# Five pairs of nodes instead of four in each PSUM tile of edge counts, and layer 0 woven in after every third tile

## The chip, the cores and the metric

The kernel runs on one core of a Trainium2 chip. The metric is the device time of one execution in microseconds (us). A core has a matrix engine (PE, whose weight loads are listed as PEld), a vector engine (DVE), a scalar engine (ACT), a general engine (POOL), and an engine that here only issues transfers (SP). Each engine works through its own queue in the order in which the program was compiled; they wait for one another by semaphores.

## The reference

The inputs are 6250 nodes of 128 features and 206,250 edges, sorted by their destination. Four graph layers follow one another, each after a layer norm and a ReLU, and each added to the residual `x`:

```python
h = relu(layernorm(x))
neighbor = segment_sum(edge_weight[:, None] * h[src], dst, N)       # layer 0
x = x + leaky_relu(neighbor @ W1.T + b1 + (h * neighbor) @ W2.T + b2, 0.2)
h = relu(layernorm(x))
agg = segment_sum(h[src], dst, N) / max(degree, 1)                  # layer 1
f = gelu(agg @ Wl.T + bl + h @ Wr.T)
...                                         # f is normalised over all nodes, f + h added to x
summed = segment_sum(x_clique[dst], src, N)                         # layer 2, a mean
x = x + (summed / max(count, 1)) @ W.T + b
h = relu(layernorm(x)) @ W_in.T + b_in                              # layer 3, a GRU cell
agg = segment_sum((h @ W_msg)[src], dst, N)
x = x + gru(agg, h) @ W_out.T + b_out
```

All four need sums over the same edges. What matters here is only the first: for each node, a sum over its edges of a weight times a row of `h`.

## The kernel before, in words

The kernel turns the list of edges into dense matrices and multiplies by them. The 6250 nodes are 49 blocks of 128 (`NB` = 49, `P` = 128). For every block of destinations two matrices over all 49 x 128 sources are made: `cnt`, how many edges lead from a source to a destination (bf16), and `edge_w`, the sum of their weights (f32). Layer 0 multiplies by `edge_w` at once; `cnt` goes to HBM (`cnt_d`, and turned by DMA for the first 25 blocks, `cntT_d`) and is read back by layers 1 to 3, in the second half of the kernel (`dense`, L820). That half is not edited.

The first half is a loop over 25 **strips** of two blocks, the last of one block (L793). For each strip:

- `prepare(k)` (L623) finds the edges of each node with gathers from HBM that POOL issues (`fetch`, L620): first a line of the sorted list (`line`), then twice up to 64 edges of a node (`dst`, `src`, `wgt`), one half after the other since the second half begins where the first one ends. DVE compares what lands (`same`, L657) and computes the next offset `off_i` (L652). The edges' fields are then turned so that an edge lies on a partition (PE, L675) and copied to `by_edge` (ACT, L677). This runs a strip or more ahead of its use.
- `count(k, ...)` (L680) makes the two matrices. A **pair** is two nodes, with up to 64 edges each, on 64 partitions each. DVE writes **one-hots** for 16 pairs at a time (`TW` = 16): `s_hot` (L695) says which of the 128 nodes of its block an edge's source is, and `k_hot` (L697, L699) which of the 49 blocks, once plainly and three times multiplied by a part of the weight. The pool `hot` has two buffers of each. PE multiplies them (L712): for each pair six products of 64 edges, three on each half of the array, into one PSUM tile `pK`. A `pK` tile is two banks, one for each node of the pair, and a pair takes 2 x 49 columns in each: 49 for the count, 49 for the weights. There are three `pK` buffers. `PW` = 4 pairs fill a tile; ACT then copies the counts to `cnt` (L726) and the weights to `edge_w` (L727).
- `layer0(k, ...)` (L743) multiplies `h0` by `edge_w`, 49 products of 128x256 f32 (L748), each of which is two instructions in the profile. It is a generator that stops after every six of them. What follows the 49 products is a chain of small steps: a copy by ACT (L753), products (L756, L762, L763), several DVE steps (L758, L765 to L771), a norm (L549), transposes of `h1` (L779) and a last product (L785, L787).

Layer 0 of one strip is **woven** into the counting of the next: whenever `count` yields, the driver asks `layer0` for its next **slice** of six products. The few lines that do it:

```python
for _ in count(k, nb, ready.pop(0), edge_w):
    next(before, None)
for _ in before:
    pass
before = layer0(k, nb, edge_w)
```

`count` yields once for each set of one-hots, which is 16 pairs or four `pK` tiles, so eight times in a strip. The tail of layer 0 comes out after the strip's last yield. In strip 0, where there is no earlier strip, `before` is the generator `norms` instead, which makes `h0`. A planner orders the instructions of each engine at compile time: near a strip's change it mixes layer 0's tail with the first tiles of the next strip, and it places `prepare`'s steps between the one-hots in DVE's queue.

When a block is complete, SP issues its write to `cnt_d` (L735), and for the first 25 blocks also seven transposing DMAs with their writes (L740, L741). `cnt` has two buffers.

Of the kernel before, what the change touches and what calls it, by code (L numbers as in the profile page):

```python
# [11 lines left out]
BF16 = mybir.dt.bfloat16  # L12
AF = mybir.ActivationFunctionType
ALU = mybir.AluOpType
DVE = mybir.EngineType.DVE

P = 128
D = 128
N = 6250
NB = -(-N // P)  # L20
# [444 lines left out]
WN = 2  # L465
H = P // WN
SB = 2
# [2 lines left out]
NS = len(STRIPS)  # L470
TW = 16
TI = 2
PW = 4
CB = 4
NQB = -(-NQ // P)
CHUNKS = [(g, min(CB, n - g)) for b, n in ((0, NQB), (NQB, NB)) for g in range(b, n, CB)]
# [9 lines left out]
def fast(ctx: ExitStack, tc: tile.TileContext, a: dict, out: bass.AP, flag: bass.AP):  # L486


    nc = tc.nc
# [35 lines left out]
    cnt_d = dram.tile([NCH, P, CB, NB * P], BF16, name="cnt_d")  # L525
# [11 lines left out]
    def flat(t):  # L537
        return t.rearrange("p b f -> p (b f)")
# [42 lines left out]
    with ExitStack() as bx:  # L581
        def pool(name, bufs):
            return bx.enter_context(tc.tile_pool(name="b_" + name, bufs=bufs))
# [12 lines left out]
        iota = keep.tile([P, P, TI], BF16, name="iota")  # L596
# [16 lines left out]
        pay, hot, work = pool("pay", 2), pool("hot", 2), pool("work", 1)  # L613
        edge = pool("edge", 2)
        cnts, turned, once = pool("cnts", 2), pool("turned", 3), pool("once", 1)
# [7 lines left out]
        def prepare(k):  # L623
# [53 lines left out]
            nc.scalar.copy(by_edge, pv)  # L677
            return by_edge

        def count(k, nb, by_edge, edge_w):  # L680


            mats = []
            for t0 in range(0, nb * P // WN, TW):
                tq = TW // TI

                def at(i, n):
                    v = by_edge[:, i, t0 : t0 + TW].rearrange("p (q o t) -> p q o t", o=1, t=TI)
                    return v.to_broadcast([P, tq, n, TI])

                def count_up(n):
                    return iota[:, None, :n, :].to_broadcast([P, tq, n, TI])

                s_hot = hot.tile([P, tq, P, TI], BF16, name="s_hot")
                nc.vector.tensor_tensor(s_hot, count_up(P), at(0, P), op=ALU.is_equal)  # L695
                k_hot = hot.tile([P, 4, tq, NB, TI], BF16, name="k_hot")
                nc.vector.tensor_tensor(k_hot[:, 0], count_up(NB), at(1, NB), op=ALU.is_equal)  # L697
                for i in range(1, 4):
                    nc.vector.tensor_tensor(k_hot[:, i], k_hot[:, 0], at(1 + i, NB), op=ALU.mult)  # L699
                for q in range(0, TW, PW):  # L700

                    pk = psum.tile([P, WN, 512], F32, name="pK", bufs=3)
                    for i in range(PW):
                        (u, t), o = divmod(q + i, TI), 2 * NB * i
                        for j in (0, 2, 3):
                            for h in range(WN):
                                r = slice(h * H, (h + 1) * H)
                                if j:
                                    to, rhs = slice(o + NB, o + 2 * NB), k_hot[r, j, u, :, t]
                                else:  # L710
                                    to, rhs = slice(o, o + 2 * NB), k_hot[r, :2, u, :, t]
                                nc.tensor.matmul(pk[:, h, to], s_hot[r, u, :, t], rhs, start=j == 0,  # L712
                                                 stop=True, skip_group_check=True)
                    n0 = (t0 + q) * WN
                    nn = PW * WN
                    if n0 % P == 0:
                        mats.append(cnts.tile([P, NB, P], BF16, name="cnt"))

                    def by_block(half):
                        v = pk[:, :, : 2 * PW * NB].rearrange("p h (i c b) -> p c b i h", c=2, b=NB)  # L720
                        return v[:, half]

                    def to_nodes(m):
                        return m.rearrange("p b (i h) -> p b i h", h=WN)

                    nc.scalar.copy(to_nodes(mats[n0 // P][:, :, n0 % P : n0 % P + nn]), by_block(0))  # L726
                    nc.scalar.copy(to_nodes(edge_w[:, :, n0 : n0 + nn]), by_block(1))  # L727
                yield
                n0 = (t0 + TW) * WN
                if n0 % P:  # L730
                    continue
                j = n0 // P - 1
                g = k * SB + j
                c, i = CHUNK_OF[g]
                nc.sync.dma_start(cnt_d[c, :, i, :], flat(mats[j]))  # L735
                if g >= NQB:
                    continue
                for q in range(0, NB, 7):
                    tt = turned.tile([P, 7, P], BF16, name="tt")
                    nc.sync.dma_start_transpose(tt, flat(mats[j][:, q : q + 7, :]))  # L740
                    nc.sync.dma_start(cntT_d[:, g, q * P : (q + 7) * P], flat(tt))  # L741

        def layer0(k, nb, edge_w):  # L743
# [49 lines left out]
        for k, nb in STRIPS:  # L793
            if k + 1 < NS:
                ready.append(prepare(k + 1))
            edge_w = edge.tile([P, NB, SW], F32, name="edge_w")
# [5 lines that stand above are left out]
# [89 lines left out]
    for g in range(0, NQB, GB):  # L891
        nb = min(GB, NQB - g)
        xq = work.tile([P, GB, D], F32, name="xq")
        n = min(NQ - g * P, nb * P)
# [80 lines left out]
    for g, nb, acc in dense(q_parts, False):  # L975
# [21 lines left out]
        h = work.tile([P, CB, D], F32, name="wb")  # L997
# [12 lines left out]
        for j in range(nb):  # L1010
            nc.tensor.matmul(pm[:, j * D : (j + 1) * D], hh[:, (g + j) * P : (g + j + 1) * P],  # L1011
                             w_msg, start=True, stop=True)
# [5 lines left out]
    for g, nb, acc in dense(m_parts, True):  # L1018
# [13 lines left out]
        r, z = gates  # L1032
# [14 lines left out]
        for j in range(nb):  # L1047
            o = po[:, j * D : (j + 1) * D]
# [13 lines left out]
def gnn_kernel(tc: tile.TileContext, a: dict, out: bass.AP):  # L1062
    nc = tc.nc
    with tc.tile_pool(name="flag", bufs=1) as keep:
        flag = keep.tile([1, 1], I32, name="flag")
        fast(tc, a, out, flag)
        found = nc.values_load(flag[0:1, 0:1], min_val=0, max_val=2 * E,
                               skip_runtime_bounds_check_because="a count of edges, each at most twice")
        with tc.If(found != E):
            general(tc, a, out)  # L1070
# [48 lines left out]
```

## Time and profile before

| | before |
|---|---|
| median of 3 runs | 2252.22 us (2247.76 to 2259.28) |
| the profiled execution's own time | 2246.41 us |
| its span, first to last instruction | 2244.6 us |
| its mean granted TensorE clock | 0.956 |
| first counting product (L712) | 53.2 us after the start |
| last strip's write of `cnt` (L735) | 1256.2 us after the start |
| strip with transposes and gathers, 234.8 to 284.3 us | 49.5 us |
| strip with gathers only, 924.2 to 971.0 us | 46.8 us |
| strip with neither, 1112.0 to 1155.6 us | 43.6 us |

A strip's time here runs from one transposition of edge fields (L675) to the next. In the profile, a group is a line of the kernel with the engine, the operation, the tiles that it writes and reads, the number of instructions, their busy time, the mean of one in ns, and the idle time of the engine just ahead of them with what ended it. A wait is read "engine, line, what it waited for: us in total, times, longest". "issue" is idle time for which the profile shows no cause. A busy share is a mean over stages with different limits, so it says little on one edit; the timeline of the stage does.

### The profile page before, as it was taken

How to read it: one execution, taken by the hardware profiler on the slowest of the kernel's cores; microseconds unless marked ns; L12 is line 12 of the kernel's file. 1: busy time of each engine (PE TensorE's matmuls, PEld its weight loads, DVE VectorE, ACT ScalarE, POOL GpSimd, SP SyncE). 2: the span in 40 equal slices, each digit the busy share in tenths (PEclk: the TensorE clock that was granted, in tenths of full speed). 3: DMA queues.
4: the chain of work that ended last, by engine and by line, in shares of the span. 5: the costliest groups of instructions: out<-in, count | busy, mean ns of one | idle time of the engine just before them, and what ended most of it. 6: DMA issues, size and time to landing. Idle time of an engine off the chain costs nothing. (4 is left out here: it accounts for less than half of the span.)

```text
span 2244.6 us, 60368 instructions
## 1 busy us (share of the span) xinstructions
PE 1959.0 (87%) x25624; PEld 1573.7 (70%) x25624; DVE 1412.1 (63%) x3349; ACT 1182.8 (53%) x2692; POOL 344.9 (15%) x377
## 2 busy tenths in 40 slices
PE   0568988888898889998999859999969989999998
PEld 0457776777777777777777747888756767778776
DVE  6687676666666666666766267777785554443443
ACT  1645555555555565665666336666645455443443
POOL 4431122211111221111100020000041110000000
PEclk9989999999999999999999979999989899997999
DMA  3687899888898222223222398878846668775774
GB/s 62 160 159 185 220 202 211 219 200 217 206 204 220 93 80 95 80 87 88 80 98 80 121 257 292 266 240 276 258 140 205 205 204 271 243 237 165 241 236 139
DMA packets 423787, 406.32 MB, mean 181 GB/s; under 512 B 191216, under 2 KB 414307, under 8 KB 417235
## 3 DMA queue, kind: packets, MB, share of 16 engines
q1 hardware_dynamic: 414883, 394.35, 61.1%
q0 software_dynamic: 5600, 6.56, 1.2%
q8 instruction: 203, 3.33, 0.6%
q10 hardware_dynamic: 3024, 1.45, 0.4%
q14 instruction: 77, 0.63, 0.1%
HBM read 227.26 MB, written 134.89 MB: 161 GB/s over the span
## 5 line engine op out<-in xcount | busy, mean ns | idle before, releaser
L726 ACT CAST cnt<-pK 128x392 bf16<-128x392 f32 x784 | 402.8, 514 | 399.5 <-PE pK L712 299.7
L748 PE MATMUL pL<-edge_w,h 128*128 128x256 f32 (+1 forms) x2450 | 610.1, 399 | 0.3 <-ACT agg L753 0.3
L712 PE MATMUL pK<-k_hot,s_hot 64*128 64x49 bf16 (+1 forms) x18816 | 429.6, 195 | 124.7 <-issue 68.9
L712 PEld LDWEIGHTS <-s_hot 64*128 64x128 bf16 x18816 | 370.6, 96 | 217.7 <-issue 166.2
L748 PEld LDWEIGHTS pL<-edge_w,h 128*128 128x128 f32 x2450 | 462.4, 200 | 66.3 <-ACT agg L753 0.5
L727 ACT COPY edge_w<-pK 128x392 f32<-128x392 f32 x784 | 410.2, 523 | 0.0
L852 PE MATMUL acc<-some,parts 128*128 128x512 f32 (+1 forms) x1456 | 374.5, 399 | 27.6 <-DVE some L847 19.7
L695 DVE TENSOR_TENSOR s_hot<-iota,by_edge 128x2048 bf16<-128x2048 bf16 x196 | 240.0, 1225 | 188.4 <-PE pK L712 180.4
L852 PEld LDWEIGHTS acc<-some,parts 128*128 128x128 f32 x1456 | 273.7, 196 | 92.9 <-DVE some L847 25.1
L699 DVE TENSOR_TENSOR k_hot<-k_hot,by_edge 128x784 bf16<-128x784 bf16 x588 | 309.5, 577 | 5.2
L841 ACT CAST others<-ring 128x1536 fp32r<-128x1536 bf16 (+3 forms) x156 | 192.4, 1233 | 206.7 <-PE acc L852 143.0
L840 DVE CAST some<-ring 128x2048 fp32r<-128x2048 bf16 (+3 forms) x156 | 166.9, 1071 | 182.8 <-PE acc L852 172.1
L852 PE MATMUL acc<-others,parts 128*128 128x512 f32 (+1 forms) x1092 | 280.1, 391 | 0.0
L847 DVE TENSOR_SCALAR_CACHE_REDUCE some<-ring 128x512 fp32r<-128x512 bf16 (+1 forms) x364 | 216.3, 652 | 63.2 <-PE acc L852 38.3
L852 PEld LDWEIGHTS acc<-others,parts 128*128 128x128 f32 x1092 | 205.2, 195 | 42.1 <-issue 0.5
L850 ACT ACTIVATE others<-ring 128x512 fp32r<-128x512 bf16 (+1 forms) x273 | 162.3, 597 | 109.9 <-issue 53.7
L774 POOL TENSOR_TENSOR xs<-xs,h 128x256 f32<-128x256 f32 (+1 forms) x25 | 26.9, 1075 | 798.0 <-ACT h L565 755.1
L852 PE MATMUL acc<-some,q_parts 128*128 128x512 f32 (+1 forms) x390 | 114.8, 422 | 31.7 <-DVE some L840 31.7
L852 PEld LDWEIGHTS acc<-some,q_parts 128*128 128x128 f32 x390 | 73.7, 204 | 53.0 <-DVE some L840 37.1
L697 DVE TENSOR_TENSOR k_hot<-iota,by_edge 128x784 bf16<-128x784 bf16 x196 | 110.2, 562 | 0.0
L657 DVE TENSOR_SCALAR_CACHE_REDUCE same<-dst,node 128x64 bf16<-128x64 int32 x50 | 13.9, 277 | 119.6 <-DMA dst<-in_dst,off_i 116.3
L852 PE MATMUL acc<-others,q_parts 128*128 128x512 f32 (+1 forms) x260 | 81.0, 422 | 0.0
(155 smaller groups left out, 1526.1 us busy)
## 6 DMA issues: line engine op xcount, KB each, us to landing
ring<-cnt_d SPq DMA_DIRECT2D x168, 896.0 KB
cnt_d<-cnt SPq DMA_DIRECT2D x49, 1568.0 KB
cntT_d<-tt SPq DMA_DIRECT2D x175, 224.0 KB
ring<-cntT_d SPq DMA_DIRECT2D x60, 640.0 KB
ring<-cnt_d SPq DMA_DIRECT2D x14, 224.0 KB
xs<-in_x SPq DMA_DIRECT2D x24, 128.0 KB
xs<-in_x SPq DMA_DIRECT2D x12, 256.0 KB
u_d<-xs SPq DMA_DIRECT2D x24, 128.0 KB
```

The source lines that it names most:

```text
L695: nc.vector.tensor_tensor(s_hot, count_up(P), at(0, P), op=ALU.is_equal)
L697: nc.vector.tensor_tensor(k_hot[:, 0], count_up(NB), at(1, NB), op=ALU.is_equal)
L699: nc.vector.tensor_tensor(k_hot[:, i], k_hot[:, 0], at(1 + i, NB), op=ALU.mult)
L712: nc.tensor.matmul(pk[:, h, to], s_hot[r, u, :, t], rhs, start=j == 0, stop=True, skip_group_check=True)
L726: nc.scalar.copy(to_nodes(mats[n0 // P][:, :, n0 % P : n0 % P + nn]), by_block(0))
L727: nc.scalar.copy(to_nodes(edge_w[:, :, n0 : n0 + nn]), by_block(1))
L748: nc.tensor.matmul(pl[:, :w], h0[:, s, :], edge_w[:, s, :w], start=s == 0, stop=s == NB - 1)
L840: nc.vector.tensor_copy(some[:, :dve, :nb], t[:, :dve])
L841: nc.scalar.copy(others[:, : step - dve, :nb], t[:, dve:])
L847: nc.vector.tensor_scalar(rhs, t[:, i], 1.0, None, op0=ALU.mult, op1=ALU.add, accum_out=total)
L850: nc.scalar.activation(rhs, t[:, i], AF.Copy, accum_out=total)
L852: nc.tensor.matmul(acc[:, :w], parts[:, q + i, j, :], rhs, start=q + i + j == 0, stop=q + i + j == last)
```

## The change

A `pK` tile takes five pairs in place of four (`PW` = 5), which is 490 of a bank's 512 columns. A block has 64 pairs (`WB`), so it is now counted in 13 tiles, twelve of five pairs and one of four, in place of 16. Tiles no longer end where one-hots do: the one-hots, still for 16 pairs each, are made by a function `one_hots` at the first pair that needs them, and a tile may read two sets.

`count` now yields after the third, sixth, ninth and thirteenth tile of a block, so the slices of layer 0 stand after 15, 30, 45 and 64 pairs in place of 16, 32, 48 and 64. There are still eight yields in a full strip. `cnt` is allocated at the start of a block. The products, their number and their order within a pair stay as they are, as do the sizes of all pools.

```diff
-PW = 4
+PW = 5
+WB = P // WN
...
+        def one_hots(by_edge, t0):
...
+            s_hot = hot.tile([P, tq, P, TI], BF16, name="s_hot")
+            nc.vector.tensor_tensor(s_hot, count_up(P), at(0, P), op=ALU.is_equal)
+            k_hot = hot.tile([P, 4, tq, NB, TI], BF16, name="k_hot")
+            nc.vector.tensor_tensor(k_hot[:, 0], count_up(NB), at(1, NB), op=ALU.is_equal)
+            for i in range(1, 4):
+                nc.vector.tensor_tensor(k_hot[:, i], k_hot[:, 0], at(1 + i, NB), op=ALU.mult)
+            return s_hot, k_hot
+
         def count(k, nb, by_edge, edge_w):
-            mats = []
-            for t0 in range(0, nb * P // WN, TW):
...
-                for q in range(0, TW, PW):
+            hots, banks = {}, range(0, WB, PW)
+            for j in range(nb):
+                g, cnt = k * SB + j, cnts.tile([P, NB, P], BF16, name="cnt")
+                for m, w0 in enumerate(banks):
+                    n = min(PW, WB - w0)
                     pk = psum.tile([P, WN, 512], F32, name="pK", bufs=3)
-                    for i in range(PW):
-                        (u, t), o = divmod(q + i, TI), 2 * NB * i
+                    for i in range(n):
+                        q, t = divmod(j * WB + w0 + i, TW)
+                        if q not in hots:
+                            hots[q] = one_hots(by_edge, q * TW)
+                        (s_hot, k_hot), (u, t), o = hots[q], divmod(t, TI), 2 * NB * i
...
-                    nc.scalar.copy(to_nodes(mats[n0 // P][:, :, n0 % P : n0 % P + nn]), by_block(0))
-                    nc.scalar.copy(to_nodes(edge_w[:, :, n0 : n0 + nn]), by_block(1))
-                yield
+                    nc.scalar.copy(to_nodes(cnt[:, :, of]), v[:, 0])
+                    nc.scalar.copy(to_nodes(edge_w[:, :, slice(j * P + of.start, j * P + of.stop)]), v[:, 1])
+                    if m + 1 == len(banks) or m % 3 == 2 and m + 2 < len(banks):
+                        yield
```

In the changed kernel the lines of this stage move: the counting products are L722 (before L712), the copies L730 and L731 (L726, L727), the one-hots L693, L695 and L697 (L695, L697, L699), and the lines of `prepare` are one higher (the comparison of a gather L658 in place of L657). From L735 on the numbers are the same.

More of the change, by code (lines that the diff above doesn't have):

```diff
@@ L678, in prepare @@
             return by_edge
-        def count(k, nb, by_edge, edge_w):
-            mats = []
-            for t0 in range(0, nb * P // WN, TW):
[L685 to L699, printed above, removed]
-                for q in range(0, TW, PW):
-                    pk = psum.tile([P, WN, 512], F32, name="pK", bufs=3)
-                    for i in range(PW):
-                        (u, t), o = divmod(q + i, TI), 2 * NB * i
-                        for j in (0, 2, 3):
@@ new lines, in one_hots, with at, count_up @@
+        def one_hots(by_edge, t0):
+            tq = TW // TI
+            def at(i, n):
+                v = by_edge[:, i, t0 : t0 + TW].rearrange("p (q o t) -> p q o t", o=1, t=TI)
+                return v.to_broadcast([P, tq, n, TI])
+            def count_up(n):
+                return iota[:, None, :n, :].to_broadcast([P, tq, n, TI])
+            s_hot = hot.tile([P, tq, P, TI], BF16, name="s_hot")
[5 more added lines that the diff above has]
+            return s_hot, k_hot
@@ new lines, in count @@
+        def count(k, nb, by_edge, edge_w):
+            hots, banks = {}, range(0, WB, PW)
[3 more added lines that the diff above has]
+                    n = min(PW, WB - w0)
+                    pk = psum.tile([P, WN, 512], F32, name="pK", bufs=3)
+                    for i in range(n):
[3 more added lines that the diff above has]
+                        (s_hot, k_hot), (u, t), o = hots[q], divmod(t, TI), 2 * NB * i
+                        for c in (0, 2, 3):
@@ L706, in count @@
                             for h in range(WN):
                                 r = slice(h * H, (h + 1) * H)
-                                if j:
-                                    to, rhs = slice(o + NB, o + 2 * NB), k_hot[r, j, u, :, t]
+                                if c:
+                                    to, rhs = slice(o + NB, o + 2 * NB), k_hot[r, c, u, :, t]
                                 else:
                                     to, rhs = slice(o, o + 2 * NB), k_hot[r, :2, u, :, t]
-                                nc.tensor.matmul(pk[:, h, to], s_hot[r, u, :, t], rhs, start=j == 0,
+                                nc.tensor.matmul(pk[:, h, to], s_hot[r, u, :, t], rhs, start=c == 0,
@@ L713, in count @@
                                                  stop=True, skip_group_check=True)
[L714 to L721, printed above, removed]
+                    of = slice(w0 * WN, (w0 + n) * WN)
@@ L723, in to_nodes @@
+                    v = pk[:, :, : 2 * n * NB].rearrange("p h (i c b) -> p c b i h", c=2, b=NB)
                     def to_nodes(m):
                         return m.rearrange("p b (i h) -> p b i h", h=WN)
-                    nc.scalar.copy(to_nodes(mats[n0 // P][:, :, n0 % P : n0 % P + nn]), by_block(0))
-                    nc.scalar.copy(to_nodes(edge_w[:, :, n0 : n0 + nn]), by_block(1))
-                yield
-                n0 = (t0 + TW) * WN
-                if n0 % P:
-                    continue
@@ L732, in count @@
-                j = n0 // P - 1
-                g = k * SB + j
+                    nc.scalar.copy(to_nodes(cnt[:, :, of]), v[:, 0])
+                    nc.scalar.copy(to_nodes(edge_w[:, :, slice(j * P + of.start, j * P + of.stop)]), v[:, 1])
+                    if m + 1 == len(banks) or m % 3 == 2 and m + 2 < len(banks):
+                        yield
                 c, i = CHUNK_OF[g]
-                nc.sync.dma_start(cnt_d[c, :, i, :], flat(mats[j]))
+                nc.sync.dma_start(cnt_d[c, :, i, :], flat(cnt))
@@ L739, in count @@
                     tt = turned.tile([P, 7, P], BF16, name="tt")
-                    nc.sync.dma_start_transpose(tt, flat(mats[j][:, q : q + 7, :]))
+                    nc.sync.dma_start_transpose(tt, flat(cnt[:, q : q + 7, :]))
                     nc.sync.dma_start(cntT_d[:, g, q * P : (q + 7) * P], flat(tt))
```

## Prediction

> **What bounds the kernel now.** I read the page's busy times and slices first: the counting stage runs from 53 to about 1290 us, and only this stage is edited. Then the groups, the list of waits, and the timelines of PE and DVE over two strips.
>
> ```profile
> PE 1959.0 (87%) x25624; PEld 1573.7 (70%) x25624; DVE 1412.1 (63%) x3349; ACT 1182.8 (53%) x2692; POOL 344.9 (15%) x377
> L726 ACT CAST cnt<-pK 128x392 bf16<-128x392 f32 x784 | 402.8, 514 | 399.5 <-PE pK L712 299.7
> L748 PE MATMUL pL<-edge_w,h 128*128 128x256 f32 (+1 forms) x2450 | 610.1, 399 | 0.3 <-ACT agg L753 0.3
> L712 PE MATMUL pK<-k_hot,s_hot 64*128 64x49 bf16 (+1 forms) x18816 | 429.6, 195 | 124.7 <-issue 68.9
> ```
>
> The stage is mostly PE: 429.6 us of counting products plus 610.1 us of layer 0 in some 1240 us. ACT waits for PE (299.7 us), not the reverse. What PE loses stands in the waits (engine, line, waited for: us, times, longest):
>
> ```profile
> PE pK L712 <- issue: 68.9, 123, 2.0
> PE pK L712 <- ACT edge_w L727: 45.5, 162, 5.2
> PE pD L779 <- ACT h L565: 20.9, 24, 3.0
> DVE same L657 <- DMA dst<-in_dst,off_i: 116.3, 40, 5.7
> ```
>
> The second line is the edit's target. In the PE timeline (start, us, then the idle time in brackets) one round of 16 pairs and six products of layer 0 looks so:
>
> ```profile
> 942.43 1.39 PE L712 MATMUL pK<-k_hot,s_hot 64*128 64x98 bf16 x72
> 944.02 0.58 PE L712 MATMUL pK<-k_hot,s_hot 64*128 64x98 bf16 x24 [0.21 <-ACT edge_w L727]
> 944.53 2.86 PE L748 MATMUL pL<-edge_w,h 128*128 128x256 f32 x12
> 947.32 1.39 PE L712 MATMUL pK<-k_hot,s_hot 64*128 64x98 bf16 x72
> ```
>
> Three tiles run through, the fourth waits 0.16 to 0.25 us for the first to be drained, the slice of layer 0 takes 2.79 us, and the round is 4.89 us. DVE, making the one-hots of a later round, meets a gather in the early part of a strip:
>
> ```profile
> 974.36 1.22 DVE L695 TENSOR_TENSOR s_hot<-iota,by_edge 128x2048 bf16<-128x2048 bf16 x1 [1.35 <-PE pK L712]
> 975.50 0.56 DVE L697 TENSOR_TENSOR k_hot<-iota,by_edge 128x784 bf16<-128x784 bf16 x1
> 979.05 0.28 DVE L657 TENSOR_SCALAR_CACHE_REDUCE same<-dst,node 128x64 bf16<-128x64 int32 x1 [2.99 <-DMA dst<-in_dst,off_i]
> 979.25 1.51 DVE L699 TENSOR_TENSOR k_hot<-k_hot,by_edge 128x784 bf16<-128x784 bf16 x3
> ```
>
> Here k_hot is late by the wait for the gather; PE does not feel it, since it needs this k_hot only at 984.60.
>
> **What the skill says.** "ScalarE: Activation LUTs", section "What ACT_TABLE_LOAD costs", gives 186 ns + 0.833 ns per element, with back-to-back instructions overlapping by about 93 ns. The trace agrees: 392 elements would be 513 ns (measured 514), copies from PSUM of 256 and 512 elements took 372 and 586 ns, a slope of 0.836, and evictions start 0.377 us apart where they take 0.48 to 0.57. "PSUM — Partial Sum Buffer", section "The four PSUM rules", gives a bank 512 fp32 columns: five pairs take 5 x 98 = 490 and fit; the kernel before shows only 392. "DVE: scalar operands, raw-bit mode, write accounting and state across instructions", section 5, calls the DVE's queue in-order; the lines above show it, k_hot behind L657.
>
> **The change, part by part.** Call a strip's time zero T, the start of its five transposes L675 (971.0 and 433.3 in two strips). Pairs cost PE 1.87/16 = 0.117 us each.
>
> Evictions. 784 pairs of copies become 49 x 13 = 637. One of 490 starts (490-392) x 0.836 = 82 ns later after its predecessor, 0.459 us. For a block ACT goes from 32 x 0.377 = 12.06 to 24 x 0.459 + 2 x 0.377 = 11.77 us. ACT is idle 299.7 us behind PE, so this 0.29 us counts for nothing by itself.
>
> Waits on the drain. Eight waits in a strip, 1.36 us (12.7 us over nine strips in 760-1180). After, groups of 3, 3, 3 and 4 tiles: the first three never meet a busy buffer. The fourth does: the first tile of 30 products ends after 0.585 us, ACT starts 0.14 later and its second copy ends 0.459 + 0.57 us after that, 1.75 us; PE is through with three tiles at 1.76. So about 0.05 us is left, twice a strip. One more deduction: the first group after a strip's change is followed by L779, which waits 0.80 us for h, a chain DVE-ACT that starts from L763 and stays. What PE saves in that group (0.20 us) and the pair that moves out of it (0.117 us) is waited for there and paid again in the 19-pair group. Net: 1.36 - 0.10 - 0.20 - 0.117 = **0.94 us a strip without gathers**.
>
> One-hots that straddle. A one-hot tile still serves 16 pairs and has two buffers, but the slices now fall after pairs 15, 30, 45, 64. Its buffer is given back at pair 16, and the refill is needed at pair 32: before, 2.79 + 1.87 + 2.79 = 7.5 us later; now one slice and 16 pairs, 2.79 + 1.87 = 4.7 us, three times in four. DVE needs 1.14 + 0.59 + 3 x 0.48 = 3.2 us, about 3.45 from release. 1.2 us of slack: free in the plain rounds (covered by PE's own rounds), not where a gather is in the way. The changed program's DVE order says where: third one-hot, then L662, L667, L670 and L655, **then the wait on the gather (L658), and only then the whole fourth one-hot**, where before s_hot and a quarter of k_hot stood ahead of it. POOL's and SP's queues keep their order.
>
> Walk for a later strip (gather lands at T+8.1). PE: pair 29 done at T+2.1, slice to 4.85, pair 44 at 6.6, slice to 9.4, pair 47 at 9.74. The third one-hot is ready at 4.2, needed at 5.1. Fourth: L658 done 8.4, s_hot and k_hot with two off_i between 8.6 to 12.05. PE stops **about 2.2 us**. But before, PE lost in the same place about 3 us to "issue" gaps, which stand beside the gathers' issue on POOL (976.72 to 983.48): 1.4 us at T+6.5 to 8.5, the rest after T+9, the second partly inside a slice. After, the first window falls into a slice and the stop. PE restarts at 12.1, does 16 pairs and a slice: 16.75 plus 0 to 1.5 us of the second window. Before, this point was T+18.46 and T+17.9. So 0 to 1.5 us less, I take 0.6, and the strip's other four groups save 0.6: **1.2 us a strip**, six strips.
>
> First half (transposes L740 run, gather lands at about T+10). The fourth one-hot is ready at 13.9, a stop of 4 us; the second gather is asked for 0.25 us later than now, and the fifth one-hot is ready at 19.8 to 20.8. PE comes there at 19.1 plus gaps; before it came at T+20.3 and T+22.1, the gaps having taken the same time. So 0 here, 0.6 saved after: **0.6 us**, 13 strips. SP's queue has room: it waited 23.2 us for ACT's cnt over eight strips.
>
> Strip 0, without layer 0, waits 15 us for ACT (11 waits) mostly behind norms: 2 us less, bounds -6 to +4 as its DVE order is reshuffled. The straddling itself adds no instruction.
>
> Sum: 4 x 0.94 + 6 x 1.2 + 13 x 0.6 + 2 = 3.8 + 7.2 + 7.8 + 2 = **21 us** off the profiled execution's 2246.4 us (span 2244.6): 0.93%. That execution lay 0.26% under the median, 2252.2; the same share of the median gives **2231 us**. Everything after 1290 us stays.
>
> **The rivals.**
> A, slower: the fourth one-hot's wait adds to the gaps instead of covering them. Place: pair 48 of each strip with gathers; price 2.2 us in six strips, 4 us in thirteen, less the 0.6 saved behind: 9.6 + 44 - 6 = +48 us, 2300. It decides as soon as the gaps lost at T+6 to T+17 reappear in full after PE's restart. For it: L657's 116.3 us and the slack of 1.2 us. Against: the gaps sit at the gathers' own times.
> B, better: PE's stop lets its instructions catch up, so the gaps go too: 1.5 us more in nineteen strips, about -50 us, 2202. For it: strips without gathers take 43.6 us, others 46 to 52.
> C, the first half gives all back, to the gathers or to the transposes' queue (DMA share 0.89 there): only 3.8 + 7.2 + 2 = 13 us, 2239. For it: there the point at pair 64 hangs on the second gather either way.
> That the tile is not larger is excluded: the program's evictions read 49x10.
>
> **Numbers.** Forecast 0.50, C 0.20, A 0.17, B 0.13. A measurement of this kernel tells about 0.5%, 11 us, from no change: under 2241 is faster, over 2263 slower. Forecast nine tenths, B whole and C in part give faster 0.65; C's rest and the forecast's edge 0.18; A 0.17. Range 2204 to 2266: it holds the forecast and C with the first half's bounds (each 0.5 us a strip), and leaves out most of A above and half of B below.
>
> **What would show it.** Waits of pK on edge_w from 45.5 to under 18 us, two a strip, each under 0.1 us. A new or larger wait of pK on k_hot (9.6 us now), about 2 us a strip late and 4 early, once per strip near T+10. "issue" before pK falling from 68.9 us. Strips without gathers at 42.6 us in place of 43.6. Eviction mean near 595 ns. Wrong if waits on k_hot pass 60 us with the issue gaps unchanged (A), or if waits on edge_w stay above 30 us: then the drain, not the count of buffers, sets the pace.

## The result, and the profile after

The changed kernel takes 2276.76 us, median of five runs (2273.17 to 2276.95), against 2256.18 of the kernel before in the same session (2247.76 to 2261.19). The ratio is 1.0092, 95% interval 1.0066 to 1.0118. It is slower by 0.9%, with an interval clear of 1: on the other side of no change from the forecast of 2231, and above the range of 2204 to 2266. The profiled execution took 2276.36 us, span 2274.6.

The groups of the page that answer to those shown of before:

```profile
PE 1933.9 (85%) x25624; PEld 1566.5 (69%) x25624; DVE 1402.4 (62%) x3349; ACT 1161.1 (51%) x2398; POOL 362.3 (16%) x377
L748 PE MATMUL pL<-edge_w,h 128*128 128x256 f32 (+1 forms) x2450 | 611.9, 399 | 0.4 <-ACT agg L753 0.3
L722 PE MATMUL pK<-k_hot,s_hot 64*128 64x49 bf16 (+1 forms) x18816 | 420.6, 198 | 153.7 <-DVE k_hot L697 129.7
```

PE is busy for 25 us less than before and the kernel takes 30 us more, so over the whole kernel the time went into waiting. In the list of waits (engine, line, waited for: us, times, longest):

```profile
PE pK L722 <- DVE k_hot L697: 129.7, 109, 6.7
DVE less L638 <- DMA line<-in_dst,at_i: 64.7, 17, 6.0
PE pD L762 <- DVE inter L758: 25.2, 23, 1.1
PE pK L722 <- ACT edge_w L731: 14.3, 16, 3.8
PE pK L722 <- issue: 5.4, 6, 3.4
```

The edit did what it says: the wait for a drained buffer fell from 45.5 to 14.3 us, and all that is left of it stands in the first 124 us. The gaps called "issue" went too, from 68.9 to 5.4. In their place stands a wait for one-hots, 9.6 us before and 129.7 now. The second line, 15.0 us before, points at one cause of it.

By strips, each measured from one transposition of edge fields (L675, now L676) to the next:

| part of the counting stage | before, us | after, us |
| --- | --- | --- |
| up to the first of the strips below | 184.9 | 176.6 |
| eight strips with transposes and gathers | 401.0 | 445.1 |
| the four after them, in which the transposes end | 199.1 | 204.2 |
| five strips with gathers only | 233.1 | 234.0 |
| the last strip with all its gathers | 50.4 | 54.1 |
| three strips with neither | 130.9 | 128.3 |
| start of the last transposition | 1199.3 | 1242.3 |

At the last transposition 43 us are lost. The eight strips lose 44, since each takes 55.6 us in place of 50.1; the strips between them and the last three lose 10 more, and 11 are gained at the two ends. One of the eight, from its start at 399.7, in the timeline of DVE (start, us, instruction, idle time before it):

```profile
415.75 1.22 DVE L693 TENSOR_TENSOR s_hot<-iota,by_edge 128x2048 bf16<-128x2048 bf16 x1
416.89 0.56 DVE L695 TENSOR_TENSOR k_hot<-iota,by_edge 128x784 bf16<-128x784 bf16 x1
423.42 0.29 DVE L638 TENSOR_SCALAR less<-line,f_node 128x128 bf16<-128x128 int32 x1 [5.97 <-DMA line<-in_dst,at_i]
423.62 1.51 DVE L697 TENSOR_TENSOR k_hot<-k_hot,by_edge 128x784 bf16<-128x784 bf16 x3
```

and of PE:

```profile
412.42 0.27 PE L722 MATMUL pK<-k_hot,s_hot 64*128 64x98 bf16 x2 [2.96 <-DVE k_hot L697]
424.24 0.22 PE L722 MATMUL pK<-k_hot,s_hot 64*128 64x98 bf16 x2 [4.09 <-DVE k_hot L697]
```

The fifth one-hot is begun at 415.75, but `less`, a comparison for a later strip, stands in DVE's queue in the middle of it. DVE waits there 5.97 us for a gather, and PE behind it 4.09. Each of the eight strips has this wait of 5.9 to 6.0 us. The first PE line is the fourth one-hot's stop, which was forecast.

Why the gather is late is in the timelines of POOL and SP. After:

```profile
415.91 1.88 POOL L621 DMA_INDIRECT line<-in_dst,at_i  x1 [1.48 <-DVE same L658]
```

```profile
417.14 0.32 SPq L735 DMA_DIRECT2D cnt_d<-cnt  x1
```

and before, with DVE's own lines last:

```profile
397.93 0.94 POOL L620 DMA_INDIRECT line<-in_dst,at_i  x1 [0.30 <-DMA f_d<-fs]
```

```profile
402.65 0.32 SPq L735 DMA_DIRECT2D cnt_d<-cnt  x1
```

```profile
402.23 0.29 DVE L637 TENSOR_SCALAR less<-line,f_node 128x128 bf16<-128x128 int32 x1 [1.70 <-DMA line<-in_dst,at_i]
402.43 1.52 DVE L699 TENSOR_TENSOR k_hot<-k_hot,by_edge 128x784 bf16<-128x784 bf16 x3
```

Before, the gather is issued at 397.93 and compared at 402.23, 4.3 us later, the longest of the eight strips, and the 1.57 MB of a block's count leave for HBM only at 402.65. After, the block ends earlier beside the gather, the write is issued 1.2 us behind it, and the gather takes 7.5 us.

The distance of 1.2 us is only half of it. The other half is the second number of the POOL lines: the issue of this gather took 1.88 us in each of the eight strips, against 0.94 before, so the write was issued before the gather's issue had ended. The records of single DMA packets in the trace give the order: the write's packets start at 417.95, and those of the gather only at 421.61, when the write's last ones start. In the next strip after the eight the write follows at 1.06 us, closer still, but the issue took 0.94 us, the gather's packets were first, and the comparison began 2.6 us after the issue. The long issues fell on DVE's one-hots: all of the 17 gather issues of more than 1.3 us in this trace ran beside one, as did all 24 before. That is a coincidence in time, and no run here parts it from a cause.

The stops seem to have a second price. In the stretch from 200 to 600 us (length, then busy us and instructions of PE, PEld, DVE, ACT and POOL, granted PE clock, DMA share, GB/s) the mean granted clock fell from 0.96 before to 0.88 after:

```profile
200.00:600.00 400.00, 351.38 (x7079) 288.13 (x7079) 270.62 (x596) 226.04 (x560) 80.05 (x93) 0.96 0.88 210
200.00:600.00 400.00, 323.02 (x6402) 270.30 (x6403) 242.85 (x537) 195.43 (x415) 81.14 (x84) 0.88 0.76 189
```

The trace's clock records show why the mean fell: in the eight strips the clock was granted at 0.5 for 31 us in 8 steps before, and for 96 us in 16 steps after, two a strip. Of these 16, 13 begin within 1.4 us of the end of a PE stop of more than 1.3 us. Of the 44 us lost, 35 are longer waits of PE and 8 are longer busy time. That the stops bring the clock down is read from this coincidence, not tested alone.

### The profile page after: what moved, and what is told of

Its sections match the earlier page's. It is cut to its first block, busy times and chain, and to the rows that moved or that the text cites. A ratio compares the mean times of both kernels' runs of the same rounds, so it can differ in the third digit from the quotient of the medians.

```text
span 2274.6 us, 59963 instructions
## 1 busy us (share of the span) xinstructions
PE 1933.9 (85%) x25624; PEld 1566.5 (69%) x25624; DVE 1402.4 (62%) x3349; ACT 1161.1 (51%) x2398; POOL 362.3 (16%) x377
## 5 line engine op out<-in xcount | busy, mean ns | idle before, releaser
L730 ACT CAST cnt<-pK 128x490 bf16<-128x490 f32 (+1 forms) x637 | 372.6, 585 | 472.8 <-PE pK L722 359.0
L722 PE MATMUL pK<-k_hot,s_hot 64*128 64x49 bf16 (+1 forms) x18816 | 420.6, 198 | 153.7 <-DVE k_hot L697 129.7
L722 PEld LDWEIGHTS <-s_hot 64*128 64x128 bf16 x18816 | 376.6, 98 | 235.7 <-issue 127.1
L852 PE MATMUL acc<-some,parts 128*128 128x512 f32 (+1 forms) x1456 | 365.6, 392 | 32.5 <-DVE some L847 20.0
L731 ACT COPY edge_w<-pK 128x490 f32<-128x490 f32 (+1 forms) x637 | 379.9, 596 | 0.0
L852 PEld LDWEIGHTS acc<-some,parts 128*128 128x128 f32 x1456 | 268.0, 191 | 95.2 <-DVE some L847 22.4
L693 DVE TENSOR_TENSOR s_hot<-iota,by_edge 128x2048 bf16<-128x2048 bf16 x196 | 240.9, 1229 | 140.5 <-PE pK L722 137.9
L697 DVE TENSOR_TENSOR k_hot<-k_hot,by_edge 128x784 bf16<-128x784 bf16 x588 | 302.9, 569 | 4.6
L847 DVE TENSOR_SCALAR_CACHE_REDUCE some<-ring 128x512 fp32r<-128x512 bf16 (+1 forms) x364 | 216.1, 651 | 59.4 <-PE acc L852 38.4
L774 POOL TENSOR_TENSOR xs<-xs,h 128x256 f32<-128x256 f32 (+1 forms) x25 | 17.9, 716 | 815.0 <-ACT h L566 815.0
L695 DVE TENSOR_TENSOR k_hot<-iota,by_edge 128x784 bf16<-128x784 bf16 x196 | 114.2, 583 | 0.0
L658 DVE TENSOR_SCALAR_CACHE_REDUCE same<-dst,node 128x64 bf16<-128x64 int32 x50 | 13.7, 275 | 106.3 <-DMA dst<-in_dst,off_i 106.3
```

The costliest lines, as they stand in the source:

```text
L730: nc.scalar.copy(to_nodes(cnt[:, :, of]), v[:, 0])
L731: nc.scalar.copy(to_nodes(edge_w[:, :, slice(j * P + of.start, j * P + of.stop)]), v[:, 1])
L847: nc.vector.tensor_scalar(rhs, t[:, i], 1.0, None, op0=ALU.mult, op1=ALU.add, accum_out=total)
L852: nc.tensor.matmul(acc[:, :w], parts[:, q + i, j, :], rhs, start=q + i + j == 0, stop=q + i + j == last)
```

## The experiments

The theory after the first look: `less`, waiting for `line` inside a one-hot, costs the eight strips (the **line theory**). Rivals: the two one-hots made back to back at a strip's end, which push L758 and so L762, PE's wait for `inter` (the **inter theory**), and the straddling one-hots with two buffers, which leave DVE less time to refill one (the **lead theory**). The letters in the expectations are each its own: the "theory L" of the first and the fourth run is the lead theory. Each ratio is against the kernel before in the same session.

**One-hots and slices on the same pairs.** Five pairs to a tile stay, but a slice comes ahead of each new one-hot, after 16, 32, 48 and 64 pairs.

```diff
                         if q not in hots:
+                            if hots and (w0 or i):
+                                yield
                             hots[q] = one_hots(by_edge, q * TW)
...
-                    if m + 1 == len(banks) or m % 3 == 2 and m + 2 < len(banks):
+                    if m + 1 == len(banks):
```

> Five pairs to a tile as in the changed kernel, but the slices of layer 0 stand where a set of one-hots ends (pairs 16, 32, 48, 64), inside a tile if need be. DVE's order is then that of the kernel before. Theory L (what costs is the shortened time between a one-hot buffer's return and its refill, with gathers in DVE's queue; the drain's gain is real): waits of pK on edge_w under 15 us (45.5 before, 14.3 after), waits of pK on k_hot at 10 us as before, waits of L764 on inter back from 25 to 9 us; time 2215 to 2240, faster than both. Rival D (the drain's gain is not real, PE only meets its issue gaps sooner): waits on edge_w gone, issue gaps up by as much, time 2250 to 2260, that of the kernel before.

Measured: 2222.94 us, ratio 0.9874 (0.9839 to 0.9909). Its waits:

```profile
PE pK L724 <- DVE k_hot L697: 69.8, 97, 7.1
PE pK L724 <- ACT edge_w L733: 34.2, 86, 4.6
DVE less L638 <- DMA line<-in_dst,at_i: 15.9, 13, 4.3
```

The time was hit, two of the three waits were not: the drain's wait is back at 34.2 us, and yet this kernel is about 2% faster than the changed one by the two ratios. So the drain is not what this difference hangs on. L762's wait returned to 0.30 us a strip, `line` to 15.9 us in all (15.0 before) and the lead to that of before, all at once, so this run doesn't part the three theories.

It shows something else, in a strip that starts at 370.1:

```profile
384.39 0.94 POOL L621 DMA_INDIRECT line<-in_dst,at_i  x1 [0.30 <-DVE at_i L634]
385.09 0.32 SPq L737 DMA_DIRECT2D cnt_d<-cnt  x1
387.54 0.28 DVE L638 TENSOR_SCALAR less<-line,f_node 128x128 bf16<-128x128 int32 x1 [0.19 <-DMA line<-in_dst,at_i]
```

The write follows the gather by 0.7 us in all eight strips, and the comparison still begins 3.0 to 3.3 us after the gather's issue, which took 0.94 us. In the ninth strip the write goes 0.8 us ahead of the gather, and it is 6.6 us. A write close behind a gather is thus not enough to make it late; in these runs it has to get ahead.

**The group of four tiles first** (4, 3, 3, 3 in place of 3, 3, 3, 4), which parts the two one-hots at the strip's end:

```diff
-                    if m + 1 == len(banks) or m % 3 == 2 and m + 2 < len(banks):
+                    if m + 1 == len(banks) or m % 3 == 0 and m > 0:
```

> The changed kernel with its groups in the order 4, 3, 3, 3 tiles, slices at pairs 20, 35, 50, 64, so that the last two one-hot buffers of a strip are given back with a slice between them. Theory I (the 1.1 us wait of L762 on inter, 25.2 us against 8.9, comes from two one-hots in a row ahead of L758, and delays the whole strip): L762 waits fall to about 9 us and the time by 10 to 20 us, to 2257 to 2267; waits of pK on k_hot stay over 100 us. Rival (that wait is hidden by later ones, above all by those on the gathers): L762 waits fall, time stays within 5 us of 2277.

Measured: 2260.79 us, ratio 1.0036 (1.0014 to 1.0058). The time lies in the inter theory's range, but not by its mechanism: L762's wait fell to 7.0 us as meant, and L779's rose from 22.5 to 38.4, so this wait mostly only moves. The gain came with the wait for `line`, which fell from 64.7 to 18.8, and stands in the eight strips (412.3 us in place of 445.1); what follows them up to the last transposition grew from 620.5 to 629.8. Waits of pK on k_hot fell to 93.3, under the 100 expected.

**No gather of the line.**

```diff
-            line = once.tile([P, P], I32, name="line")
-            fetch(line, "dst", at_i)
+            line = line_once
```

> The changed kernel without the gather of line: the comparison less reads a constant tile, so the edges found are not those of the nodes, and the count of edges that decides on the second program is set by hand. Theory G (in the first eight full strips the fifth one-hot waits 5.9 us in DVE's queue behind L638, which waits for line): waits of pK on k_hot fall from 130 to 70 to 90 us, strips of the first half from 55.3 to 50 to 51.5 us, time 2230 to 2245. Rival T (the first half is held by the transposes and their queue, and line is only the nearest wait): strips stay over 54 us, the wait turns up at cnt or elsewhere, time 2265 or more.

Measured: 2197.34 us, ratio 0.9756 (0.9722 to 0.9790); the eight strips take 388.9 us. The gain on the changed kernel is about twice the expected one: 56 us in the eight strips and 13.5 at the beginning. L762's wait for `inter` stayed at 25.4 us, so the inter theory can't explain the loss. The line theory can, but with the gather go its load and the edges that it finds.

**Eight pairs to a one-hot, four buffers:** `TW` = 8 in place of 16, `pool("hot", 4)`.

> The changed kernel with one-hots for 8 pairs and four buffers of each in the same space, so that a buffer is given back after 8 pairs and refilled for use 24 pairs later. Theory L (lead time): a refill has 24 pairs and one or two slices, 5.6 to 8.4 us, for about 1.8 us of DVE work; waits of pK on k_hot fall from 130 to under 60 us, time 2225 to 2250. Rival Q (DVE's queue order is what costs: behind the gather's comparison stands the next one-hot whatever its size): waits on k_hot stay over 100 us, time 2270 or more; twice as many DVE instructions also cost about 0.3 us for 16 pairs.

Measured: 2244.30 us, ratio 0.9973 (0.9952 to 0.9995). The time was hit; waits of pK on k_hot, at 98.9 us, were not. The five strips with gathers only fell to 42.2 to 43.8 us, but the first half's stayed at 53.8 to 55.1 with 78.7 us of waits of `less`. The lead is worth something where the line is not in the way.

**The line compared and counted on GpSimd**, so that DVE's queue has no wait for it:

```diff
-            nc.vector.tensor_scalar(less, line, n0, None, op0=ALU.is_lt)
-            nc.vector.tensor_reduce(c, less, axis=mybir.AxisListType.X, op=ALU.add)
-            nc.vector.tensor_add(off, at, c)
+            nc.gpsimd.tensor_scalar(less, line, n0, None, op0=ALU.is_lt)
+            w = P // 2
+            while w:
+                nc.gpsimd.tensor_tensor(less[:, :w], less[:, :w], less[:, w : 2 * w], op=ALU.add)
+                w //= 2
+            nc.gpsimd.tensor_tensor(off, at, less[:, :1], op=ALU.add)
```

It was put into four kernels: the changed one, the one with aligned slices, the one with small one-hots, and the one before.

> The changed kernel with the comparison and the count of line (L638, L640, L642) done by POOL in place of DVE; every gather is still issued. Theory G (it is the place of this wait in DVE's queue that costs): strips of the first half from 55.3 to 48 to 50 us as in e3, waits of pK on k_hot 70 to 100 us, time 2200 to 2225. Rival H (the gather itself costs, by its traffic or by the edges that e3 no longer found, wherever its result is read): strips stay at 53 us or more, time 2255 or more.

> e1 with line compared on POOL. In e1 DVE waited only 15.9 us for line. Theory G: 5 to 20 us less than e1, 2203 to 2218. Rival: in e1 this wait was hidden behind the second gather of dst, time within 4 us of e1's 2223.

> e4 with line compared on POOL. In e4 the strips of the second half had come down to 42.2 to 43.8 us while those of the first half stayed at 54 to 55 us behind waits for line (78.7 us). Theory G: first-half strips at 46 to 49 us, waits of pK on k_hot under 50 us, time 2165 to 2200, the fastest of all. Rival T (first-half strips are held by the transposes, DMA share near 0.9): they stay at 52 us or more, time 2225 or more.

> The kernel before with line compared on POOL, so that the edit of e5 is seen without the change. DVE waited 15.0 us for line there, ten times. Theory G (the wait costs only where the one-hots have lost their lead): 0 to 15 us less than the kernel before, 2236 to 2251. Rival H (it costs in any kernel): 40 us less or more, below 2212.

| kernel | us | ratio | eight strips, us | they start at |
| --- | --- | --- | --- | --- |
| changed, line on GpSimd | 2231.58 | 0.9894 (0.9863 to 0.9926) | 392.1 | 190.1 |
| aligned, line on GpSimd | 2242.32 | 0.9937 (0.9917 to 0.9956) | 402.3 | 188.4 |
| small one-hots, line on GpSimd | 2207.62 | 0.9782 (0.9749 to 0.9816) | 386.5 | 203.8 |
| before, line on GpSimd | 2237.67 | 0.9930 (0.9908 to 0.9953) | 398.0 | 195.0 |

Here the gather is still made, and the eight strips of the changed kernel fall by 53 us with the comparison off DVE's queue, those of the kernel before by 3. The line theory is shown, and the 44 us of the loss are accounted for. Of the four expected times only the last came; the strips of the first and third kernel came as expected too. The beginning became 13.5 us longer in the changed and in the aligned kernel, where nine GpSimd operations follow each of the gathers of `line`, eleven of which come before the first of the eight strips. The aligned kernel, which had little wait for `line` to lose, became slower. The first and last lines are the edit without the wait: 2231.58 against 2237.67, a gain of 6 us, with intervals that overlap.

**The count written later.** In the changed kernel the write of a block's count goes behind the first three transposes of that block:

```diff
-                nc.sync.dma_start(cnt_d[c, :, i, :], flat(cnt))
                 if g >= NQB:
+                    nc.sync.dma_start(cnt_d[c, :, i, :], flat(cnt))
                     continue
                 for q in range(0, NB, 7):
...
+                    if q == 14:
+                        nc.sync.dma_start(cnt_d[c, :, i, :], flat(cnt))
```

> The changed kernel with one DMA moved: the write of a block's count to cnt_d is issued after the first three transposes of that block in place of before them, some 7 us later. In the changed kernel's profile the gather of line is issued at 415.91, the cnt_d write (1.57 MB) at 417.14, and the gather lands at about 423.4, 7.5 us after its issue; in the kernel before the same gather goes at 397.93, lands at about 402.2, 4.3 us after, and the cnt_d write goes only at 402.65. Theory W: the earlier block end has put the write on top of the gather, and the write costs the gather some 3 us. Then the wait of less for line falls from 5.9 to 2.5 to 3.5 us in each of the eight first-half strips, the strips from 55.5 to about 52.5, and the kernel is 18 to 30 us faster than the changed kernel: 2247 to 2259. Theory N: the gather is late from the transposes or from general traffic: the wait stays above 5 us and the time within 8 us of the changed kernel's 2277.

Measured: 2235.78 us, ratio 0.9931 (0.9908 to 0.9954), 1.6% (36 us) below the changed kernel's ratio. In the strip that starts at 379.2, DVE and then SP:

```profile
398.52 0.29 DVE L638 TENSOR_SCALAR less<-line,f_node 128x128 bf16<-128x128 int32 x1 [2.23 <-DMA line<-in_dst,at_i]
398.72 1.52 DVE L697 TENSOR_TENSOR k_hot<-k_hot,by_edge 128x784 bf16<-128x784 bf16 x3
```

```profile
399.84 0.59 SPq L743 DMA_DIRECT2D cnt_d<-cnt  x1
```

The gather was issued at 394.75, so it took 3.8 us in place of 7.5, and the wait 2.23 in place of 5.97. Its issue still took 1.88 us, and the write went 5.1 us behind it, 3.2 us later in the strip than in the changed kernel and not the 7 expected. The eight strips fell from 445.1 to 402.7 us. So the write is what made a gather with a long issue late, and the wait is theory W's; the aligned kernel shows that the same write is harmless behind a short issue. The time fell by more than the 30 us that W had allowed. In the eight strips 26 of the 42 us are shorter waits of PE and 17 are shorter busy time: the granted clock of the stretch from 200 to 600 us also came back, to 0.95, with one step at 0.5 a strip and one stop.

**The same move in the kernel before**, as a control.

> The kernel before with the same move as e9: the cnt_d write after the block's first three transposes. In the kernel before the write is issued after the line gather has landed (402.65 against 402.2), so it slows no gather that VectorE waits for. If e9's 41 us came from taking the collision away, this kernel changes by less than 10 us: 2242 to 2262. If the late write helps any kernel of this form, it gains 20 us or more: 2215 to 2235.

Measured: 2221.47 us, ratio 0.9813 (0.9788 to 0.9838). By time this is the second reading: the move helps this kernel too. By place it is another gain: 6 us in the eight strips, 8 at the beginning, 4 after the last transposition, and 5 in the five strips with gathers only, whose writes the edit leaves where they were. Its groups and its wait:

```profile
L750 PE MATMUL pL<-edge_w,h 128*128 128x256 f32 (+1 forms) x2450 | 594.3, 391 | 0.6 <-ACT agg L755 0.3 <-issue 0.3
L712 PE MATMUL pK<-k_hot,s_hot 64*128 64x49 bf16 (+1 forms) x18816 | 422.5, 195 | 122.9 <-DVE k_hot L699 71.8 <-ACT edge_w L727 48.0 <-issue 1.6
```

Against before, the waits ahead of the counting products fell by 1.8 us (124.7 to 122.9) and the busy time of the two kinds of products by 22.9 (610.1 + 429.6 to 594.3 + 422.5). In the changed kernel the same move took 27.5 us of those waits (153.7 to 126.2), 21.4 of busy time and 42 in the eight strips. So the kernel before had a loss of its own in PE's products, which this move, or the one of the line, also takes away in part. Most of it is in layer 0's slices: 19 of those before took 3.5 to 5.4 us in place of 2.86, each on a step of the granted clock to 0.5, and 11 do so here. The "issue" gaps, 68.9 us before, are 1.6 here, and 71.8 us of waits for k_hot have their place. This fits with gaps that had covered one-hots late in any case, but is not shown one by one.

It also gives the edit a fair price. With the write late in both, five pairs take 2235.78 us against 2221.47: 14 us more, or 27 by the two ratios, which are of different sessions; the start of the last transposition differs by 14.5 us (1193.5 against 1179.0). A strip with gathers only takes 46.8 us with five pairs (234.1 in five strips) and 45.6 with four (228.1).

**Towards a faster kernel,** from small one-hots: the count of the first three lines back on DVE, the line gathered one strip ahead, and the late write.

> The kernel with one-hots of eight pairs, four buffers, and the line's count on GpSimd (2207.6), but with the count of the first three strips back on VectorE. There the nine GpSimd operations stood on the path of the beginning: the fourth strip's transposes began at 203.8 against 190 with the count on GpSimd and 16-pair one-hots and 176.6 without. Theory: 10 to 16 us come back at the beginning and nothing else moves: 2190 to 2199. Rival: the beginning is set by the gathers of dst, not by the count: 2203 to 2210.

> One-hots of eight pairs in four buffers, the line's count on VectorE, but the line of a strip gathered in the preparation of the strip before it, in two buffers: the wait of less for line goes without any work added to GpSimd. Theory: less waits under 10 us in all, the first-half strips fall to 47 to 49 us and the beginning stays short: 2180 to 2200. Rival: the junk count and the second line come to stand elsewhere in VectorE's queue and stop it there: 2205 to 2245.

> One-hots of eight pairs in four buffers (2244.3, of which nine first-half strips take 54 to 55 us with 78.7 us of waits of less for line) with the cnt_d write after the first three transposes. Theory: the collision was in this kernel too, and the nine strips fall by 5 to 7 us each, with nothing added to GpSimd: 2185 to 2205. Rival: the write then meets the gathers of dst, which come earlier here, and half of it is lost: 2215 to 2240.

Measured: 2206.88 us, ratio 0.9803 (0.9767 to 0.9839): no gain, in the rival's range, and the beginning shortened by 5 us only, since the planner puts the first eleven of these counts there and eight of them stayed on GpSimd. Then 2249.17, ratio 0.9995 (0.9979 to 1.0012), above the rival's range: the planner put the gather back to just ahead of its comparison and 0.2 to 1.7 us behind the count's write, it takes 5.7 to 7.9 us there, and `less` waits 65.0 us for it. And 2197.51, ratio 0.9729 (0.9704 to 0.9754), as expected: the eight strips at 388.2 us, 6 less each, and the lowest ratio of all, 2.7% under the kernel before. Against the changed kernel with the late write alone (0.9931) the smaller one-hots are worth 2%, which fits with a price of the lead of its own. In its waits `less` costs half of the 78.7 us that it cost with the early write:

```profile
PE pK L722 <- DVE k_hot L697: 53.6, 33, 5.2
DVE less L638 <- DMA line<-in_dst,at_i: 36.2, 17, 3.3
```

## Why the prediction was wrong, by its steps

**Evictions.** Right. A copy of 490 elements took 588 and 599 ns (about 595 forecast; an estimate of 594 comes from the formula of the Trainium skill, "ScalarE: Activation LUTs", section "What ACT_TABLE_LOAD costs"), and ACT's busy time fell by 21.7 us, worth nothing.

**Waits on the drain.** Right in sign and, in part by luck, in size in the strips without gathers: 43.57, 43.56 and 43.75 us became 43.14, 42.91 and 42.22, on average 0.87 less (0.94 forecast). The wait of 1.40 us went to zero there; the walk had kept 0.10 of it. The deductions were others than the walk's. Not seen: two one-hots are released without a slice between, at pairs 112 and 128; DVE makes them back to back ahead of L758, and L762 waits 1.10 us a strip in place of 0.30. Not in the sum either: the busy time of the counting products fell by 0.8 us a strip, which makes up for it.

**The fourth one-hot, late by the gather.** The stop was sized right: 2.6 to 4.5 us in the eight strips, 4 forecast, and 1.9 to 3.2 in the six later ones, 2.2 forecast. What it takes away was over-rated: the gaps went, and their going was no gain. The six later strips lost 4.5 us, 3.6 of them in the last, where 7.2 were to be saved: 12 us off the sum. Why the gaps were worth nothing stays open, as said above.

**The beginning.** It gained 8.3 us up to the first of the eight strips, where 2 were forecast for strip 0. The same 8 us are gained by the late write with four pairs to a tile, so it need not be the drain's.

**The fifth one-hot "is ready at 19.8 to 20.8"**, counted from the strip's start. This is the step that failed. It was ready at 423.62 + 1.51 - 399.7 = 25.4, since `less` stood in DVE's queue inside it and the gather of `line` took 7.5 us. The walk doesn't name this gather at all. Its time for the fifth one-hot is that of before, where `less` stood in the same place and the one-hot was ready at 402.43 + 1.52 - 383.7 = 20.3; so the wait for `line` was carried over from before without a reason. The walk had not asked what the shortened block sends out next, the write of 1.57 MB, nor whether it would get ahead of the gather. With the write moved, the one-hot was ready at 398.72 + 1.52 - 379.2 = 21.0. That this kernel took 2235.78 us, inside the range and 5 us from the forecast, is luck: its gains are not those of the sum, as the control says. The term was 13 x 0.6 us of gain; eight of these strips lost 5.5 each.

**The rivals.** A had the sign and the engine (k_hot past 60 us), but its mechanism, gaps that come back, didn't happen: they went, and in the eight strips the larger of the two stops waits for another gather. B was right that the gaps go too, and wrong that this is a gain. C looked at the pair where it happened and saw the second gather of `dst`, not the one of `line`. That POOL's and SP's queues keep their order was true; their distance in time changed, and with it the order in which their packets reached the DMA engines.

**What stays open.** What the "issue" gaps of the kernel before are, and what brings its steps of the clock: five pairs, the line on GpSimd and the late write each take the gaps away, and the last two shorten the products too (to 1020.4 and 1016.8 us from 1039.7), though none was made to. Why an issue on POOL takes twice as long beside a one-hot. And what follows the last transposition is 13 us shorter after (2274.6 - 1242.3 against 2244.6 - 1199.3), where the forecast had no change: part of the counting stage's 43 us is given back there, for no cause that these runs show.

## What to carry to other kernels

When an edit makes a stage shorter, ask for each transfer what is now issued beside it, how long its own issue takes and which of the two gets there first, and look in the in-order queue for the instruction that waits for the slower one: a comparison of 0.29 us for a later strip held up the one-hot of this one. Before counting a gap as a gain, see whether another wait ends just behind it. And price an edit against a kernel with the suspected wait cured in both: here one such pair still showed a loss of 14 to 27 us, and another a gain of 6 that is not clear of noise.

## What the hardware showed that was not expected

In the eight strips the same 128-partition gather was compared 7.4 to 7.5 us after its issue began when a write of 1.57 MB was issued 1.2 us behind it and its issue on POOL took 1.88 us, 3.5 to 3.9 us with the same long issue and the write 5 us behind, and 3.0 to 3.3 us with an issue of 0.94 us and the write only 0.7 us behind. So in these runs the gather is late where the write's packets get ahead of its own, and how long POOL takes over the issue helps to decide that.

Two stops of PE in each strip, of 3 to 5 us, went with a mean granted clock of 0.88 over 400 us, where one stop a strip had 0.95. Moving one write later by 2 to 3 us in a strip went with 1.6 and 1.9% of two kernels, in the second mostly at other places than the write's.
